# A four-layer kernel: norms and gates of the second layer as filling work, joined gate products, and loads and clears issued earlier

## The chip, the cores and the metric

The kernel runs on one core of one Trainium2 chip. The metric is device time in microseconds (us) of one execution, and for the kernel before it is a median over 17 runs. A separate profiled execution gives the trace that the line numbers, durations and windows come from. The engines are named PE (TensorE, matrix products; PEld is its weight load), DVE (VectorE), ACT (ScalarE), POOL (GpSimd) and SP (SyncE, which here only issues DMAs).

## The reference, cut to what matters

The input is 16 sequences of 256 tokens with 128 channels, 4096 tokens in all. Four layers follow one another, each of the form

```
xn = layernorm(x)
x  = x + attn(xn) + ffn(xn)
```

The first layer (called layer 0 here) has a recurrence over the 256 tokens of a sequence: a 64 x 128 memory matrix per sequence is updated and normalised at every token. The change is mostly in the second (layer 1):

```
# attn, on the 16 sequences of 256 tokens
n  = channel_group_norm(xn, 16 groups)        # over (8 channels x 256 tokens)
q, k = l2_normalize(n @ qw.T), l2_normalize(n @ kw.T);  v = n @ vw.T
y  = 16 heads of 8: ((q k^T) * scale * gamma_h^(i-j), causal) v
x1 = xn + y @ ow.T + ob
x2 = x1 + silu(channel_group_norm(x1) @ w1.T + b1) @ w2.T + b2

# ffn: four experts, a number of them per token between 1 and 4
h      = relu(xn @ dp_w1 + dp_b1)
ent    = softplus(h @ dp_w2 + dp_b2)
k_tok  = clip(round(1 + clip((ent - 0.5) / 1.5, 0, 1) * 3), 1, 4)
logits = xn @ gate_w + gate_b
w      = softmax over the k_tok largest logits, 0 elsewhere
out    = sum_e w_e * (relu(xn @ ew1_e + eb1_e) @ ew2_e + eb2_e)
```

The third layer (layer 2) has a windowed attention with a memory and eight experts of fixed capacity; the fourth (layer 3) softmax attention and eight experts with one expert per token. Layer 2 adds into a DRAM table `acc_d` and layer 3 scatters rows into a DRAM table `xs_d`. Both tables have to be zero before that.

## The kernel before, in words

X, the running sum, stays on the chip as 32 tiles of 128 tokens. The layers run one after another.

**Layer 0** ends with a recurrence of 16 chunks of 16 steps (index c for the chunk, t for the step), a chain that passes between DVE and ACT, with the other engines beside it; a chunk takes about 35 us. For each chunk SP issues loads from DRAM: VA and KT (lines 726 and 730), CZ (699), CR (712), and small tables tw (717). An output projection (L1162, added into X at L1166) follows.

**Layer 1** (lines 1170 to 1551) starts with its weights: 26 DMAs on ACT's own queue (L1180 to L1217). Then it makes the layer norm of all 32 tiles in 8 groups of 4 (L1233 to L1240): `kit.stats` gives mean and variance on DVE (L122, L123) and the reciprocal root on POOL (L112, L113), `kit.normalise` writes xn on DVE (L143), PE transposes four tiles (L151), and ACT copies them to xnT (L1240).

After that a loop over the 32 tiles is a pipeline with its order written out by hand. For DVE, PE and ACT the order of the program text is the order of execution (`manual_schedule`); for POOL and SP a scheduler decides. Tile n passes these stages:

- `normed(g)`, once for each four tiles: a channel group norm (L1242 to L1271) in pieces, with small products pgn (L1251, L1260) and a power on POOL (L1263).
- `project(n)`: the product pq for q, k and v (L1349), squares on ACT (L1356), ss on POOL (L1359, L1360), qk on DVE (L1364), and the outer products kv on POOL (L1373).
- `retain(n, h)` for two halves of heads: the product pk with a triangular table (L1392; for odd tiles also with ones on the tile before, L1391), then pr and y on DVE (L1396, L1399). There are two buffers of pk.
- `turn(n)`: a transpose of y on PE into pyt (L1407).

Between these stages the loop calls `some(k)`, which takes k steps from a generator, the *filler*: 7 steps in each of the 33 iterations and 2 ahead of the loop. In the kernel before, the filler is first `gates()` and then eight `tail(g)`. `gates()` has 25 steps: for each of 8 groups one product ph (L1279, 64 columns, relu into hd by ACT at L1281), four products pl of xnT with gate_w (L1285) and four of hd with dp_w2 (L1288). The rest is one block: a copy of pl to lg (L1292), and a chain of small DVE and ACT operations to the weights W (L1294 to L1332). The 25th step transposes W (pw, L1337), copies it to WT and sends it to DRAM as w_d (L1339).

`tail(g)` has 24 steps for four tiles. It begins with DMAs that read w_d back, spread over the partitions as WB (L1414) and as w4 (L1416). Then come the experts' up products (L1425), relu on ACT (L1427), a multiplication by WB on DVE (L1428), down products (L1433), the attention's output and its feed-forward part, and the addition into X (L1491). `tail(g)` may not start before tile 4g + 3 is turned. An operation on DVE that follows a filler product (the multiplication by WB, say) is put into a list `St.later` and is emitted with the next step. What is left of the filler after the loop is drained.

**Preparation of layer 2.** `prepare2` is called before layer 1. Its loads are on SP's queue, its small memsets on POOL. At its end (L1619 to L1627) it makes a tile of zeros on POOL and clears `acc_d` (2048 KB) and `xs_d` (2967 KB) with two DMAs on SP's queue (L1622).

Of the kernel before, what the change touches and what calls it, by code (L numbers as in the profile page):

```python
# [9 lines left out]
F32 = mybir.dt.float32  # L10
# [14 lines left out]
NCH = T // CH  # L25

# [57 lines left out]
class Kit:  # L84


    def __init__(self, ctx, tc, tables):
# [12 lines left out]

        self.mv3 = pool.tile([P, NT, 2], F32, name="mv3")
# [13 lines left out]
    def stats(self, pool, src, n):  # L115
# [10 lines left out]
        return mv, rstd  # L126

# [38 lines left out]
def layer0(tc, I, kit, X):  # L166
# [3 lines left out]
    with ExitStack() as ctx:  # L170
# [462 lines left out]
        with ExitStack() as c2:  # L633
# [237 lines left out]
            def chunk(c):  # L871
# [53 lines left out]
                for t in range(CH):  # L925
# [35 lines left out]
                    if t in (9, 10):  # L961
                        shares(t - 9, SA, CR)
                    elif c > 1 and t in (4, 5, 6, 11, 12, 13, 14):
                        beside(320)
                    if c < 2 and t < 8 and t % 2:
                        gram_out(1, 4 * c + t // 2, Run.pgs, 0)
# [203 lines left out]
def layer1(tc, I, kit, X):  # L1170
    nc = tc.nc
    H, DH, E = 16, 8, 4
    with ExitStack() as ctx:
        wp = ctx.enter_context(tc.tile_pool(name="l1_w", bufs=1))
        big = ctx.enter_context(tc.tile_pool(name="l1_big", bufs=1))
# [3 lines left out]
        for i, n in enumerate(("qw", "kw", "vw")):  # L1179
            nc.scalar.dma_start(wqkv[:, i, :], I[f"L1_attn_{n}_T"])  # L1180
        ow = wp.tile([P, D], F32, name="ow")
        nc.scalar.dma_start(ow, I["L1_attn_ow_T"])
        col = {}
        for n in ("norm_g", "norm_b", "ob", "ffn_norm_g", "ffn_norm_b"):
            col[n] = wp.tile([P, 1], F32, name="c_" + n)
            nc.scalar.dma_start(col[n], I["L1_attn_" + n].unsqueeze(1))
        w1 = wp.tile([P, 2 * D], F32, name="w1")
        nc.scalar.dma_start(w1, I["L1_attn_w1_T"])
        w2 = wp.tile([P, 2, D], F32, name="w2")
        nc.scalar.dma_start(w2, I["L1_attn_w2_T"].rearrange("(k p) d -> p k d", p=P))  # L1190
        b1 = wp.tile([P, 2], F32, name="b1")
        nc.scalar.dma_start(b1, I["L1_attn_b1"].rearrange("(k p) -> p k", p=P))
        b2 = wp.tile([P, 1], F32, name="b2")
        nc.scalar.dma_start(b2, I["L1_attn_b2"].unsqueeze(1))

        gw = wp.tile([P, E], F32, name="gw")
        nc.scalar.dma_start(gw, I["L1_ffn_gate_w"])
        gb = wp.tile([P, E], F32, name="gb")
        nc.scalar.dma_start(gb, row_bcast(I["L1_ffn_gate_b"]))
        dw1 = wp.tile([P, 64], F32, name="dw1")  # L1200
        nc.scalar.dma_start(dw1, I["L1_ffn_dp_w1"])
        db1 = wp.tile([64, 1], F32, name="db1")
        nc.scalar.dma_start(db1, I["L1_ffn_dp_b1"].unsqueeze(1))
        dw2 = wp.tile([64, 1], F32, name="dw2")
        nc.scalar.dma_start(dw2, I["L1_ffn_dp_w2"])
        db2 = wp.tile([P, 1], F32, name="db2")
        nc.scalar.dma_start(db2, row_bcast(I["L1_ffn_dp_b2"]))
        ew1 = wp.tile([P, E, 2 * D], F32, name="ew1")
        nc.scalar.dma_start(ew1, I["L1_ffn_ew1"].rearrange("e d h -> d e h"))
        ew2 = wp.tile([P, E, 2, D], F32, name="ew2")  # L1210
        for e in range(E):
            nc.scalar.dma_start(ew2[:, e], I["L1_ffn_ew2"][e].rearrange("(k p) d -> p k d", p=P))
        eb1 = wp.tile([P, E, 2], F32, name="eb1")
        with nc.allow_non_contiguous_dma(reason="1024 biases"):
            nc.scalar.dma_start(eb1, I["L1_ffn_eb1"].rearrange("e (k p) -> p e k", p=P))
        eb2 = wp.tile([E, D], F32, name="eb2")
        nc.scalar.dma_start(eb2, I["L1_ffn_eb2"])  # L1217
# [8 lines left out]
        kvp = ctx.enter_context(tc.tile_pool(name="l1_kv", bufs=3))  # L1226
# [5 lines left out]


        for g in range(8):
            sl = slice(4 * g, 4 * g + 4)
            mv, rstd = kit.stats(tmp, X[:, sl, :], 4)
            xn = tmp.tile([P, 4, D], F32, name="xn")
            kit.normalise(xn, X[:, sl, :], mv, rstd, 4)
            pn = kit.transpose4(ps2, xn, "h")
            nc.scalar.copy(xnT[:, 512 * g : 512 * g + 512], pn)  # L1240

# [31 lines left out]
        def gates():  # L1273

            pl = ps.tile([P, NT, 8], F32, name="pl", tag="f")
            for g in range(8):
                cols = slice(512 * g, 512 * g + 512)
                ph = ps2.tile([64, 512], F32, name="ph", tag="h")
                nc.tensor.matmul(ph, dw1, xnT[:, cols], start=True, stop=True)  # L1279
                hd = tmp.tile([64, 512], F32, name="hd")  # L1280
                nc.scalar.activation(hd, ph, AF.Relu, bias=db1)  # L1281
                yield
                for i in range(4):
# [1616 lines left out]
```

## Time and profile before

| | us |
|---|---|
| median of 17 runs | 1955.23 |
| lowest and highest of them | 1950.46, 1959.74 |
| profiled execution, its own time | 1955.67 |
| its span in the trace | 1953.7 |
| last part of layer 0's sum into X (L1166) | 656 |
| first copy to xnT (L1240) | 674.72 |
| first product pq (L1349) | 686.09 |
| last product pl | 734.9 |
| transpose of W (L1337) | 746.44 |
| last addition into X of layer 1 (L1491) | 1016.4 |

The page gives for each engine the share of the span in which it was busy: PE 77%, DVE 69%, ACT 42%, POOL 33%. These are averages over four layers with different limits, so a change in one layer is read from that layer's rows. A *window* is a stretch of the span, with each engine's busy time (and number of instructions), the mean clock that PE was granted (1.00 is full speed), the share of time in which the DMA engines were busy, and GB/s. The *chain of waits* is followed back from the last instruction: at each step it goes to what released the instruction, or to the instruction before it on its engine. SP's *timeline* lists when it issues DMAs: start, duration of the issue, line, and destination<-source; the transfer itself comes later.

### The profile page before, as it was taken

The page shows a single profiled execution, that of the slowest core. Times are in us where ns is not written, and L with a number is a line of the kernel's source. Part 1 is how long each engine was busy: PE and PEld are TensorE (multiplying, and loading weights), DVE is VectorE, ACT ScalarE, POOL GpSimd, SP SyncE. Part 2 cuts the span into 40 slices and gives each one's busy share as a digit, 9 for nine tenths or more (in the row PEclk, how much of TensorE's full clock was granted, in tenths as well). Part 3 has the DMA queues.
Part 4 walks back from the last instruction along what each step waited for, and adds up shares of the span by engine and source line. Part 5 has one row for each costly group of instructions (what it writes and reads, how often), then busy time and mean ns, then how long its engine had stood idle before and what let it go on. Part 6 is the DMA issues. An engine that isn't in the chain of part 4 may idle for free.

```text
span 1953.7 us, 26353 instructions
## 1 busy us (share of the span) xinstructions
PE 1510.9 (77%) x8176; PEld 920.6 (47%) x8176; DVE 1340.3 (69%) x4656; ACT 822.5 (42%) x1908; POOL 636.5 (33%) x901
## 2 busy tenths in 40 slices
PE   6676666766765598999988888687887289999995
PEld 3355455554654453444434454344444145555553
DVE  5688999888898537887855567654366256666663
ACT  3554554555555113232324345343443044454443
POOL 4332313122121223343413031566672713333310
PEclk9676767777676668999998999898888589999998
DMA  3130001000000451101102000022222313333314
GB/s 106 26 86 21 14 12 48 17 12 16 11 16 3 99 96 52 37 22 44 22 0 43 4 1 1 18 44 50 36 57 82 109 57 91 103 101 93 107 54 120
DMA packets 114978, 94.43 MB, mean 48 GB/s; under 512 B 35463, under 2 KB 97799, under 8 KB 114599
## 3 DMA queue, kind: packets, MB, share of 16 engines
q1 hardware_dynamic: 94172, 64.20, 13.0%
q0 software_dynamic: 13056, 26.21, 5.4%
q10 hardware_dynamic: 7610, 2.35, 0.5%
q8 instruction: 65, 1.06, 0.2%
q14 instruction: 75, 0.61, 0.1%
HBM read 55.65 MB, written 37.01 MB: 47 GB/s over the span
## 4 chain that ended last, share of the span: by engine, by line
PE 44%; DVE 11%; POOL 5%; issue 4%; DMA 2%; ACT 1%; another core or an unknown queue 0%; ACTq 0%; SPq 0%; POOLq 0%; DVEq 0%
PE pM L2606 6%; PE pc L2619 3%; PE ph L2282 3%; PE pf L1433 3%; PE pf L2265 3%; DVE mx L2781 3%; PE ph L1425 2%; PE pf L2708 2%; PE pk L1392 2%; PE tr L151 2%; PE ph L2701 2%; PE pk L1391 1%; POOL tok L2168 1%; DVE x L143 1%; PE pE L2606 1%
## 5 line engine op out<-in xcount | busy, mean ns | idle before, releaser
L2781 DVE TENSOR_REDUCE mx<-pM 128x4 f32<-128x1024 f32 x128 | 155.2, 1216 | 128.4 <-PE pE L2606 84.9
L2606 PE MATMUL pM<-ke,qe 31*128 31x256 f32 x1024 | 157.9, 436 | 69.8 <-DVE mx L2781 32.3
L2786 ACT ACTIVATE PT<-pE 128x1024 f32<-128x1024 f32 x128 | 130.4, 1024 | 170.1 <-PE pE L2606 168.3
L2606 PEld LDWEIGHTS pM<-ke,qe 31*128 31x128 f32 x1024 | 96.7, 201 | 112.6 <-DVE mx L2781 54.9
L2606 PE MATMUL pE<-qe,ke 32*128 32x256 f32 x1024 | 148.5, 410 | 0.6 <-ACT PT L2786 0.4
L940 ACT ACTIVATE SA<-e,y 16x1 f32<-16x1 f32 x256 | 74.9, 292 | 131.9 <-DVE e L939 104.6
L976 ACT ACTIVATE iR<-SA,A,CR 16x1 f32<-16x1 f32 x240 | 92.5, 386 | 53.2 <-DVE A L945 38.1
L808 PE MATMUL pP<-KB,M 128*128 128x64 f32 x224 | 59.7, 402 | 49.9 <-ACT M L690 49.9
L1131 POOL TENSOR_SCALAR KA<-KT,aS 128x128 f32<-128x128 f32 x128 | 74.8, 603 | 64.1 <-ACT aS L1103 64.1
L2606 PEld LDWEIGHTS pE<-qe,ke 32*128 32x128 f32 x1024 | 93.0, 189 | 4.5 <-ACT PT L2786 2.5
L740 POOL COPY KB<-K 64x256 f32<-64x256 f32 x30 | 11.9, 397 | 248.1 <-PE pP L808 247.3
L1373 POOL TENSOR_TENSOR kv<-qk,v 128x1024 f32<-128x1024 f32 x32 | 65.9, 2059 | 40.9 <-PE pf L1433 10.9
L808 PEld LDWEIGHTS pP<-KB,M 128*128 128x128 f32 x224 | 49.7, 297 | 59.0 <-ACT M L690 59.0
L1427 ACT ACTIVATE e<-ph,eb 128x512 f32<-128x512 f32 x64 | 44.1, 689 | 76.8 <-PE ph L1425 76.1
L2720 POOL DMA_INDIRECT ya_d<-yo,own x46 | 45.8, 995 | 80.8 <-DVE yo L2718 73.8
L2619 PE MATMUL pc<-PT,ve 128*32 128x256 f32 x1024 | 71.1, 397 | 0.0
L1399 DVE TENSOR_REDUCE y<-pr 128x64 f32<-128x512 f32 x64 | 69.1, 1080 | 2.2
L292 PE MATMUL pn<-tab,xn 128*128 128x128 f32 x32 | 14.3, 460 | 70.7 <-POOL xn L284 70.7
L1392 PE MATMUL pk<-kv,tab 128*128 128x512 f32 x128 | 68.4, 626 | 0.0
L1425 PE MATMUL ph<-xnT,ew 128*128 128x512 f32 x128 | 66.8, 603 | 0.0
L1433 PE MATMUL pf<-e,ew 128*128 128x512 f32 x128 | 64.1, 592 | 0.0
L945 DVE SCALAR_TENSOR_TENSOR A<-CR,e,A 16x33 f32<-16x33 f32 (+3 forms) x240 | 57.6, 240 | 8.5
(603 smaller groups left out, 4202.9 us busy)
## 6 DMA issues: line engine op xcount, KB each, us to landing
WB<-w_d SPq DMA_DIRECT2D x8, 1024.0 KB
c_d<-cs SPq DMA_DIRECT2D x16, 512.0 KB
ew<-in_L_ffn_W SPq DMA_DIRECT2D x16, 256.0 KB
xs_d<-zero SPq DMA_DIRECT2D x1, 2967.0 KB
xt<-xs_d POOLq DMA_DIRECT2D x23, 129.0 KB
xrow_d<-XN SPq DMA_DIRECT2D x4, 548.0 KB
X<-in_x SPq DMA_DIRECT2D x4, 512.0 KB
VA<-v_d SPq DMA_DIRECT2D x64, 32.0 KB
```

Source lines behind the costliest of these rows:

```text
L808: nc.tensor.matmul(Run.pP[p // 4][:, o : o + 64], M[:, p, :], KB[:, p].rearrange("q h k -> q (h k)"), start=p % 4 == 0, stop=False, skip_g ...
L940: nc.scalar.activation(s, e, AF.Sqrt, bias=y, scale=-1.0)
L976: nc.scalar.activation(iR, s, AF.Sqrt, bias=A[:, 17:18], scale=SB[:, t, 17:18])
L1131: nc.gpsimd.tensor_scalar(KA[:, p, :], KT[:, p, :], Run.aS[:, p : p + 1], None, ALU.mult)
L1392: nc.tensor.matmul(pkf, kit["triu"], St.kv[n][:, hs], start=i == 0, stop=True)
L1399: nc.vector.tensor_reduce(St.y[n][:, hh], pr.rearrange("p h e f -> p h f e"), AX.X, ALU.add)
L1425: nc.tensor.matmul(ph, ew1[:, e, k * P : (k + 1) * P], xg, start=True, stop=True)
L1433: nc.tensor.matmul(pf, ew2[:, e, k, :], he[q], start=False, stop=False)
L2606: nc.tensor.matmul(out[:, k, i, :], A[rows, s, c + i * P : c + i * P + P], B[rows, s, c : c + T], start=True, stop=True,)
L2619: nc.tensor.matmul(St.pc[32 * r : 32 * r + 32, s % 2, :], VEs[b % 2][:, k, 4 * s + r, :], St.PT[b, s][:, r, k, :], start=k == 0, stop=k == 1,)
L2781: vec.tensor_reduce(St.mx[bm][:, h0 : h0 + 2, :], pM, AX.X, ALU.max)
L2786: act.activation(St.PT[b, s][:, r0 : r0 + 2], pE, AF.Exp, scale=scale)
```

## The change

1. *Norms.* Only group 0's layer norm stays ahead of the loop. The moments are now made by an existing function (`kit.next_moments`, which leaves mean, reciprocal root and the negative of their product, the last with two small POOL operations more than before), the rows by `norm_rows` (two tiles on DVE, two on ACT), and the transposes and the copy by `norm_turn`. Groups 1 to 7 become the first 27 steps of the filler, `norms()`. `normed(g + 1)` starts at the second tile of a group of four rather than at the first.
2. *Gates.* gate_w is joined to dp_w1 as four more columns; ph has 68 rows, 64 through relu and 4 through identity with gate_b as bias, as two ACT operations. dp_w2 becomes a table of 68 x 5: an identity block for the four logits and dp_w2 as fifth column. So a group takes one ph and four pl rather than one and eight, and the addition of gate_b on DVE falls away. The products of a group come one round after its ph. The chain to W is cut by seven `yield`s, so the loop's own work comes between its pieces. `gates()` has 18 steps of products and 8 of the chain.
3. *Weights of layer 1.* The 26 DMAs are on SP's queue. The order in which layer 1's buffers are laid out changes, so that the weights take room that the recurrence's `work` buffers had. In SP's order they stand behind the last chunk's KT load. The joined tables take a few POOL operations (two memsets and a copy).
4. *Clears.* Both tables and the tile of zeros belong to the kit now. `kit.clear_rooms` is called in chunk 3 of layer 0's recurrence at step 9: a DVE memset of the zeros (128x129), and the two DMAs on SP's queue, between two tw loads.
5. *yT.* The copy of pyt to yT is made as soon as the fourth tile of a group is turned, with four buffers, not when the tail starts.

The diff, cut to its core:

```diff
+    def clear_rooms(self):
+        nc = self.nc
+        nc.vector.memset(self.zero, 0.0)
+        for rows, n, w in (
+            (self.acc_d.rearrange("(n p) c -> p n c", p=P), NT, D),
+            (self.xs_d.rearrange("(k p) c -> p k c", p=P), L3_NTL * L3_TS // P, D + 1),
+        ):
+            nc.sync.dma_start(rows, self.zero[:, 0:w].unsqueeze(1).to_broadcast([P, n, w]))
...
+                    if (c, t) == (3, 9):
+                        kit.clear_rooms()
...
-            nc.scalar.dma_start(wqkv[:, i, :], I[f"L1_attn_{n}_T"])
+            nc.sync.dma_start(wqkv[:, i, :], I[f"L1_attn_{n}_T"])
...
+        dw1 = wp.tile([P, 64 + E], F32, name="dw1")
+        nc.sync.dma_start(dw1[:, 0:64], I["L1_ffn_dp_w1"])
+        nc.sync.dma_start(dw1[:, 64:], I["L1_ffn_gate_w"])
...
+        dw2 = wp.tile([64 + E, E + 1], F32, name="dw2")
+        nc.gpsimd.memset(dw2[0:64], 0.0)
+        nc.gpsimd.memset(dw2[64:], 0.0)
+        nc.gpsimd.tensor_copy(dw2[64 : 64 + E, 0:E], kit.ident[64 : 64 + E, 64 : 64 + E])
+        nc.sync.dma_start(dw2[0:64, E : E + 1], I["L1_ffn_dp_w2"])
...
-        for g in range(8):
-            sl = slice(4 * g, 4 * g + 4)
-            mv, rstd = kit.stats(tmp, X[:, sl, :], 4)
-            xn = tmp.tile([P, 4, D], F32, name="xn")
-            kit.normalise(xn, X[:, sl, :], mv, rstd, 4)
-            pn = kit.transpose4(ps2, xn, "h")
-            nc.scalar.copy(xnT[:, 512 * g : 512 * g + 512], pn)
+        def norm_rows(g):
+            xn = xns[g] = tmp.tile([P, 4, D], F32, name="xn")
+            for i in range(4):
+                n = 4 * g + i
+                if i % 2 == 0:
+                    nc.vector.tensor_scalar(
+                        xn[:, i, :], X[:, n, :], kit.mv3[:, n, 0:1], kit.rs3[:, n : n + 1], ALU.subtract, ALU.mult
+                    )
+                else:
+                    nc.scalar.activation(
+                        xn[:, i, :], X[:, n, :], AF.Identity, scale=kit.rs3[:, n : n + 1], bias=kit.nb3[:, n : n + 1]
+                    )
+        def norms():
+            for g in range(1, 10):
+                if g < 8:
+                    kit.next_moments(tmp, X, g)
+                yield
+                if 2 <= g < 9:
+                    norm_rows(g - 1)
+                yield
+                if g >= 2 and g < 9:
+                    norm_turn(g - 1)
+                yield
...
-            for g in range(8):
+            for g in range(9):
+                if g < 8:
...
+                    ph = ps2.tile([64 + E, 512], F32, name="ph", tag="h")
+                    nc.tensor.matmul(ph, dw1, xnT[:, cols], start=True, stop=True)
+                    hd = tm2.tile([64 + E, 512], F32, name="hd")
+                    nc.scalar.activation(hd[0:64], ph[0:64], AF.Relu, bias=db1[0:64])
+                    nc.scalar.activation(hd[64:], ph[64:], AF.Identity, bias=db1[64:])
                 yield
-                for i in range(4):
-                    ts = slice((4 * g + i) * P, (4 * g + i + 1) * P)
-                    nc.tensor.matmul(pl[:, 4 * g + i, 0:E], xnT[:, ts], gw, start=True, stop=True)
+                if g > 0:
+                    for i in range(4):
+                        n = 4 * g - 4 + i
+                        nc.tensor.matmul(pl[:, n, 0 : E + 1], last[:, i * P : (i + 1) * P], dw2, start=True, stop=True)
                 yield
...
         def filler():
+            yield from norms()
             yield from gates()
...
+            kit.next_moments(tmp, X, 0)
+            norm_rows(0)
+            norm_turn(0)
             for _ in normed(0):
                 pass
...
-                if j == 0 and g + 1 < 8:
+                if j == 1 and g + 1 < 8:
                     norm = normed(g + 1)
...
-    clear(acc_d.rearrange("(n p) c -> p n c", p=P), NT, D)
-
-    xs_d = dram.tile([L3_NTL * L3_TS, D + 1], F32, name="xs_d")
-    clear(xs_d.rearrange("(k p) c -> p k c", p=P), L3_NTL * L3_TS // P, D + 1)
```

## The prediction

> **What bounds the kernel now.** I read the page's head and clock row first, then the chain of waits around the seam of layers 0 and 1, the rows of the xnT copy, the windows from 656 us on, and SyncE's timeline for the clears.
>
> ```profile
> span 1953.7 us, 26353 instructions
> ...
> PEclk9676767777676668999998999898888589999998
> ```
>
> The profiled execution took 1955.67 us, 0.44 above the median of the 17 runs; the sum is made against it. Each digit of the clock row is 48.8 us; layer 1 (656 to 1016.4 us) begins in the 14th, and the 14th and 15th stand at 6 where its later ones stand at 9.
>
> ```profile
> 656.74 2.58 DMA wqkv<-in_L_attn_vw_T
> ...
> 672.20 2.49 DMA fl<-in_L_attn_fgate
> 674.72 0.59 ACT xnT L1240
> ...
> 686.09 1.65 PE pq L1349 x2
> ...
> 746.01 0.39 DVE W L1332
> 746.44 0.47 PE pw L1337
> ```
>
> The chain (start, duration) runs through weight transfers until ScalarE makes its first copy at 674.72, then through the other norms to the first projection at 686.09, and at 735 to 746 through the gate chain.
>
> ```profile
>   DMA fl<-in_L_attn_fgate: 28.7, 1
> ```
>
> This is the idle time before that copy. ScalarE was issuing 26 weight DMAs (655.85 to 674.6). The first norm's rows were ready at 660, so this wait is pure queueing.
>
> ```profile
> core 0: us, PE busy (x) PEld busy (x) DVE busy (x) ACT busy (x) POOL busy (x), PEclk, DMA share, GB/s
> 656.00:686.00 30.00, 9.32 (x36) 6.79 (x36) 20.23 (x111) 4.59 (x8) 12.61 (x65) 0.50 0.72 148
> 686.00:698.00 12.00, 11.91 (x26) 5.91 (x27) 2.59 (x10) 3.15 (x12) 5.78 (x6) 0.50 1.15 221
> 698.00:735.00 37.00, 37.00 (x146) 21.58 (x144) 13.57 (x26) 6.01 (x17) 6.43 (x7) 0.76 0.32 37
> 714.00:738.00 24.00, 24.00 (x100) 13.15 (x99) 9.38 (x17) 6.18 (x17) 5.08 (x6) 0.86 0.00 1
> 754.00:1016.00 262.00, 256.75 (x680) 115.77 (x679) 206.05 (x443) 82.46 (x219) 91.80 (x93) 1.00 0.12 30
> ```
>
> PE is the bound from 686 to 735 (37.00 of 37 busy) but slow: 0.50, then 0.76. From 754 it is 98% busy at full clock.
>
> ```profile
> 681.00 0.53 SPq L1622 DMA_DIRECT2D acc_d<-zero  x1
> 681.58 5.43 SPq L1622 DMA_DIRECT2D xs_d<-zero  x1
> 747.24 0.33 SPq L1339 DMA_DIRECT2D w_d<-WT  x1
> 748.84 0.36 SPq L1414 DMA_DIRECT2D WB<-w_d  x1
> ```
>
> The two clears move 5.0 MB; the DMA view shows their traffic ending near 706, about 25 us after issue. The last two lines are the way of the gate weights into WB.
>
> **The change, part by part.** A filler step is one piece of second work; a loop iteration (one tile of 128 tokens) takes seven, and two lie before the loop.
>
> *Start of layer 1.* The 26 issues leave ScalarE and seven norms leave the front. What remains before the first pq, from 656.3: moments 1.1, 45 POOL memsets (end 657.2, they stay), rsqrt 1.3, two rows on DVE 0.56 beside two on ACT, four transposes 1.2, copy 0.59, then the group norm (DVE pieces 3.2, two small products, pow 0.7): about 11.7 with waits. First pq at 668 instead of 686.1. The weights now stand in SP's queue after the KT load of the last chunk and wait only for that chunk's products, so they are issued about 617 to 632, with 25 us to land; the recurrence hides them. SP's later preparation of layer 2 started at 655.84, when its buffers came free, and is no later. Bounds: 666 to 676.
>
> *Part A, 27 norm steps* (3.6 iterations). DVE: 7 x (1.1 + 0.56) = 11.6; retain 2 x (0.684 + 1.081) and qk 0.68 per tile, 3.4 tiles: 14.3; one group norm 3.2; together 29. PE at full clock: a tile costs 3.8 (pq 0.81, triangular pk 1.8, half of the tiles another 1.9 of pk, pyt 0.3), x 3.6 = 13.6, transposes 7 x 0.6 = 4.2: 18; at half clock 36. POOL: 3.6 x (kv 1.96 + ss 0.93) + 7 x (1.27 + two small 0.5) = 23, with one wait for SP's late fl load (about 670) ahead of the fourth rsqrt. So A lies between 29 (DVE) and 42 (half clock and waits); since 656 to 698 ran at 0.50, I take 35.
>
> *Part B, 18 product steps* (2.57 iterations). The 32 logit products (64 passes, L1285) go; the logits ride as four more columns in ph and pl. ACT gets 8 more activations (at most 0.68 each; ACT was busy 9 of 49 us here, so hidden). PE at full clock: 8 ph x 1.0 + 8 quads of pl x 0.98 + 2.57 x 3.8 = 25.6; at half clock 51. With the clock between the rows 0.76 and 0.86, 0.81, B is 31.5. Bounds 26 and 48.
>
> The Trainium skill, "TensorE: Matmul & The Clock Gate", Part 1, What's actually happening, says that about 3.4 us of sustained work release the throttle. The trace differs: PE was 11.91 of 12 busy at 0.50, and the measurement decides. By the rule B would be near 26 and the time about 1943.
>
> *Part C, 8 steps of the gate chain* (1.14 iterations). Before, it ran as one block from lg at 735.8 to pw at 746.44 with PE idle. It loses one add (0.29); between its pieces now stand 1.14 tiles of DVE work (4.8) and pieces of a group norm (1.4): 10.3 + 6.2 = 16.5 to pw. Bounds 13 (DVE busy alone: 6 + 6.2, and some waits) and 18.
>
> *A new wait.* WB lands about 9 us after w_d's issue (747.24 to the WB traffic's end, 756). Before, tails began with tile 5 and two tiles' work lay between. Now eight tiles are turned, tail 0 starts at once, and its first e*WB stands on DVE with the next pr and y behind it; with two pk buffers PE stops too. PE has about 5 us of other work: 4 us (0 to 6).
>
> *The rest.* Before: 753.6 to 1016.4 = 262.8 for tiles 5 on and eight tails. Now tails start at about 7.3, back to back (before, 4 of 28 steps were empty): 2.3 tiles x 3.8 = 8.7 less, 254.1. The yT copy is the same, only earlier.
>
> *Clears in chunk 3.* One DVE memset (POOL took 0.21 for the same form) may sit on the recurrence: 0.2. The DMAs are issued near 215, land near 241 at the seam's 25.5 us; the tw loads queued behind them on SP and the rings are needed near 247.5. Hidden by chunk 4's first eight steps, with 6 us over; without it up to 8. SP issues in order and some completion counters are shared, so CR (222.79 before), KT (233.38) and CZ (238.30) behind the clears also wait for their landing and leave near 241; KT is first read by POOL's KA after 250 and CZ with the next chunk, so they stay hidden too. At 681 they delayed nothing that PE waited for, so their leaving gains 0.
>
> The Trainium skill, "DMA: Bandwidth & Descriptors", Issuing engines are not separate DMA queues, says that another issuing engine saves only the sequencer's time, usually small. Here that time was 28.7 us of idle ScalarE, so the trace disagrees with "small"; if the rule held, pq would come near 681 and the time near 1962.
>
> Sum: 668 + 35 + 31.5 + 16.5 + 4 + 254.1 = 1009.1, with the memset 1009.3, against 1016.4: 7.1 earlier. Layers 2 and 3 keep their work. 1955.67 - 7.1 = 1948.6.
>
> **Rivals.** (1) *The clock stays at half*, the other side. For: 0.50 over 656 to 698 with PE full in the last 12, and again in 702 to 714; A is DVE-bound and leaves PE gaps. Against: 0.86 from 714, while a cold PE is itself full in A. A 40, B 48: end 1030.8, time 1970. It decides from A + B = 73.6, a mean clock in B under 0.66.
> (2) *The clears hold the recurrence*: they land more than 32 us after issue. For: 134 to 175 GB/s in the second half of their transfer. Against: other loads shared that. Up to +8: 1956.
> (3) *All is better hidden*: A 29, B 26, C 14, no WB wait: end 991, time 1931. For: the 98% of 754 to 1016. Against: the clock rows.
> (4) *The start isn't freed*, because SP, which issues in order, reaches the weights late: pq near 676, time 1957. Against: in its timeline of before SP issued nothing from 612 to 641.
>
> **How the numbers follow.** Chances: forecast 0.50, (1) 0.18, (2) 0.08, (3) 0.16, (4) 0.08. What a measurement here can tell from no change is about 0.2%, 3.9 us. The forecast's own range is 1939 to 1957 (A 31 to 38, B 28 to 37): some 0.42 of it faster, 0.06 same, 0.02 slower. Adding (3) as faster, (1) as slower but 0.02, (2) and (4) spread over the three: faster 0.63, same 0.14, slower 0.23. The range takes in all of (3) and (2) and (4) and the lower half of (1): 1930 to 1966.
>
> **What would show it.** First pq near 668 with no ACT wait on a DMA; layer 1's last X add near 1009; PE busy 60% or more but DVE fuller in 668 to 703; clock of 0.8 in 703 to 735; a DVE wait on WB's DMA once, near 752 to 758; chunk 4 of the recurrence as long as chunk 5; pl with one shape only. Wrong if the first 70 us after pq take over 77 at a low clock, if KT or tw loads show up as releasers near 247, or if POOL's rsqrt ends the waits of A.

## The result and the profile after

The changed kernel takes 1964.03 us (median of 8 runs, 1961.99 to 1965.92), the kernel before 1955.63 (47 runs, 1949.82 to 1959.77). The ratio is 1.0045, 95% interval [1.0034, 1.0055]: 0.45% slower. The forecast was 1948.6, faster, and both the sign and the size were wrong; the time lies inside the range of 1930 to 1966 and near its upper end.

The traces agree on where it happens. Layers 2 and 3, from the last X add of layer 1 to the end of the span, take 937.3 us before (1953.7 - 1016.4) and 937.8 after (1962.6 - 1024.8). Layer 0's last add starts at 655.8 before and 656.6 after. So the loss is in layer 1: from that add to its own last X add it took 360.6 us and takes 368.2.

The head and the clock row of the page of the kernel after:

```profile
span 1962.6 us, 26250 instructions
...
PEclk9676767777676688989998999898988589999997
```

The chain of waits of the kernel after, from layer 0's end to the first tail (start, duration, what):

```profile
662.45 0.59 ACT xnT L1274
...
668.36 1.66 PE pq L1401 x2
...
715.37 0.86 PE ph L1327 x2
...
754.38 0.49 PE pw L1389
...
757.13 7.96 DMA w<-w_d
765.14 2.07 PE pf L1509 x2
```

The first projection comes at 668.4, 17.7 us earlier than before, as forecast. But the first product of the gates stands at 715.4, 47 us later; that was to be 35. The gate weights W are transposed at 754.4 (8 us later than before), and after it PE waits for w4 to come back from DRAM.

The windows of the kernel after that belong to the norm steps, the product steps, and two stretches further on (columns as in the header):

```profile
core 0: us, PE busy (x) PEld busy (x) DVE busy (x) ACT busy (x) POOL busy (x), PEclk, DMA share, GB/s
668.00:715.00 47.00, 31.23 (x68) 14.44 (x69) 33.27 (x110) 13.96 (x46) 27.24 (x46) 0.59 0.12 15
715.00:737.00 22.00, 22.00 (x106) 13.22 (x104) 11.72 (x23) 13.98 (x32) 5.77 (x6) 1.00 0.00 0
...
825.00:845.00 20.00, 17.88 (x45) 8.39 (x44) 13.95 (x35) 4.53 (x14) 5.14 (x7) 0.83 0.10 25
...
870.00:880.00 10.00, 9.34 (x23) 4.25 (x22) 8.43 (x25) 2.91 (x8) 4.48 (x5) 0.83 0.00 1
```

Beside the norm steps neither PE (31 of 47) nor DVE (33 of 47) is full, at a clock of 0.59. The product steps then run at full clock without a gap; in the kernel before, 698 to 735 stood at 0.76. In 825 to 845 and 870 to 880 PE has gaps and its clock drops, in a part of the layer where the kernel before was 98% busy at 1.00.

The waits of the kernel after between 735 and 772 (total, times, longest):

```profile
DVE e L1482 <- DMA WB<-w_d: 6.4, 1, 6.4
...
PE pf L1509 <- DMA w<-w_d: 4.7, 1, 4.7
```

This is the new wait behind W: DVE's first multiplication by WB, and PE's product with w4.

SP's timeline of the kernel after, around the clears in chunk 3:

```profile
214.14 0.38 SPq L143 DMA_DIRECT2D acc_d<-zero  x1
214.58 5.01 SPq L143 DMA_DIRECT2D xs_d<-zero  x1
219.68 14.15 SPq L734 DMA_DIRECT2D tw<-rec_d  x2
234.11 1.72 SPq L747 DMA_DIRECT2D KT<-kh_d  x4
235.94 0.36 SPq L729 DMA_DIRECT2D CR<-rec_d  x1
241.36 0.31 SPq L716 DMA_DIRECT2D CZ<-rec_d  x1
```

CZ waits 5.0 us for the landing of the second clear and leaves at 241.4 (238.3 in the kernel before). CR leaves at 235.9 instead of 222.8, now behind the KT loads; the wait found for it is 0.9 us on DVE and none on a clear, so the prediction's reading that CR and KT would be held until 241 did not come true. The waits of the recurrence (36 to 600 us) name one load in the kernel after, GB with 1.1 us (2.2 before), and neither KT nor tw.

### The profile page after: what moved, and what is told of

It is laid out like the page before. It is cut to its first block, busy times and chain, and to the rows that moved or that the text cites. A ratio compares the mean times of both kernels' runs of the same rounds, so it can differ in the third digit from the quotient of the medians.

```text
span 1962.6 us, 26250 instructions
## 1 busy us (share of the span) xinstructions
PE 1501.7 (77%) x8112; PEld 913.2 (47%) x8112; DVE 1341.9 (68%) x4640; ACT 833.7 (42%) x1932; POOL 636.3 (32%) x919
## 4 chain that ended last, share of the span: by engine, by line
PE 42%; DVE 13%; issue 4%; POOL 4%; DMA 2%; ACT 1%; another core or an unknown queue 0%; SPq 0%; POOLq 0%; DVEq 0%; ACTq 0%
PE pM L2651 6%; PE pc L2664 3%; PE pf L1487 3%; DVE mx L2826 3%; PE ph L1479 3%; PE ph L2327 2%; PE pf L2310 2%; PE pf L2753 2%; PE pk L1444 2%; PE ph L2746 2%; PE tr L168 2%; DVE x L160 1%; POOL tok L2213 1%; PE pk L1443 1%; PE pE L2651 1%
## 5 line engine op out<-in xcount | busy, mean ns | idle before, releaser
L757 POOL COPY KB<-K 64x256 f32<-64x256 f32 x30 | 11.8, 394 | 247.1 <-PE pP L825 246.3
L1425 POOL TENSOR_TENSOR kv<-qk,v 128x1024 f32<-128x1024 f32 x32 | 64.8, 2024 | 35.6 <-DVE qk L1416 19.5
L1482 DVE TENSOR_TENSOR e<-e,WB 128x512 f32<-128x512 f32 x64 | 45.8, 715 | 28.5 <-ACT e L1481 21.9
```

## The experiments

The runs were made on several chips, on which the kernel before took medians of 1921 to 1960 us; what follows layer 1 takes 902 to 905 us on some and 934 to 940 on others, whatever the kernel. Layer 1 itself does not depend on the chip in the one case that shows it: front, filler and chain are the same to 0.1 us in the changed kernel and in tails_aligned, which ran on different ones. So times are compared as ratios to the kernel before on the same chip, and the stages by their lengths in each trace. All lengths in us, from one trace for each kernel, with marks rounded to 0.1. "Front" is from the start of layer 0's last add to the first pq, "filler" from there to the copy of pl to lg (norm steps, if any, and product steps), "chain" from lg to pw, "rest" from pw to the last X add of layer 1.

| run | front | filler | chain | rest | layer 1 | ratio [95%] |
|---|---|---|---|---|---|---|
| before | 30.3 | 49.7 | 10.6 | 270.0 | 360.6 | 1 |
| after | 11.8 | 68.7 | 17.3 | 270.4 | 368.2 | 1.0045 [1.0034, 1.0055] |
| norms_ahead | 24.6 | 26.8 | 19.5 | 273.9 | 344.8 | 0.9907 [0.9877, 0.9938] |
| tails_aligned | 11.8 | 68.7 | 17.3 | 261.5 | 359.3 | 0.9966 [0.9945, 0.9987] |
| weights_only | 50.2 | 50.8 | 10.7 | 272.5 | 384.2 | 1.0125 [1.0086, 1.0165] |
| gates_only | 30.8 | 29.2 | 11.8 | 274.3 | 346.1 | 0.9911 [0.9874, 0.9948] |
| norms_dense | 11.7 | 49.3 | 15.7 | 273.8 | 350.5 | 0.9971 [0.9956, 0.9985] |
| moments_ahead | 22.0 | 61.9 | 17.3 | 270.3 | 371.5 | 1.006 [1.0043, 1.0077] |
| chain_block | 24.6 | 26.8 | 12.8 | 277.8 | 342.0 | 0.9922 [0.9905, 0.9938] |
| weights_clears | 31.3 | 55.4 | 10.6 | 270.1 | 367.4 | 1.0037 [1.0023, 1.0052] |
| pl_twice | 24.5 | 33.8 | 12.9 | 277.7 | 348.9 | 0.9948 [0.9931, 0.9964] |
| gates_beside | 44.4 | 2.6 | 10.5 | 291.3 | 348.8 | 0.9938 [0.9921, 0.9955] |
| rank_beside | 44.4 | 2.6 | 7.5 | 293.0 | 347.5 | 0.9926 [0.9904, 0.9948] |
| xnT_passes | 24.6 | 38.2 | 10.5 | 273.5 | 346.8 | 0.9942 [0.9921, 0.9964] |
| no_lag | 24.6 | 46.1 | 10.6 | 280.9 | 362.2 | 1.0019 [1.0, 1.0038] |
| front_and_rank | 25.9 | 25.0 | 10.8 | 277.4 | 339.1 | 0.9889 [0.9863, 0.9915] |

A filler with more steps leaves fewer tiles for the rest, so "filler" and "rest" are to be read together: 7 steps are one tile, 3.8 us of PE at full clock.

### norms_ahead: the norms out of the filler

```diff
-            kit.next_moments(tmp, X, 0)
-            norm_rows(0)
-            norm_turn(0)
+            for g in range(9):
+                if g < 8:
+                    kit.next_moments(tmp, X, g)
+                if g > 0:
+                    norm_rows(g - 1)
+                    norm_turn(g - 1)
...
         def filler():
-            yield from norms()
             yield from gates()
```

> The changed kernel with all eight layer norms ahead of the loop again (moments and rows in the changed form, each group's rows and transposes one group behind its moments) and no norm steps in the filler. Theory 1, the norm steps in the filler are dear (47 us for 3.57 iterations where the tiles alone take 3.57 x 3.8 = 13.6) and through their 27 steps they push the tails out of their phase: first pq near 678 (13 us of DVE moments and rows, then 7 for the group norm), tail 0 starts with tile 4 as in the kernel before, last X add of layer 1 near 1000, time about 1939 (1933 to 1946). Rival: the joined products, the split chain or the moved loads cost the time: last X add at 1018 or later, time 1957 or more.

Measured: first pq at 680.1, last X add at 1000.3, ratio 0.9907. Theory 1 gave 678 and 1000, and the rival falls. Taking this one part back (with the norms in the changed kernel's form, each group's moments ahead of the rows of the group before) makes layer 1 23.4 us shorter than in the changed kernel and 15.8 shorter than in the kernel before. The front is 12.8 us longer than in the changed kernel, and the filler 41.9 shorter.

### tails_aligned: the tails in one phase

```diff
-                while St.turned < 4 * g + 3:
+                while not (St.turned >= 4 * g + 3 and (St.ended or St.fresh and St.turned % 4 == 3)):
```

(`St.fresh` is set for the one step after a turn, `St.ended` after the loop.)

> The changed kernel, but a tail starts only at the step at which it could start in the kernel before (right after the last tile of a group of four is turned), so tails come every 28 steps, one group later, and two of them are drained after the loop. Theory 1: back-to-back tails run against the tile stages in changing phases, and that costs the 10 us that the stretch 825 to 912 has too much: tile spacing of 35 us per four tiles all along, PE 98% busy at full clock from 765 on, last X add near 1014, time about 1953 (1949 to 1957). Rival: what is lost there is not the phase but work that must be done anyway, and the second drained tail costs 3 us more: last X add 1025 to 1029, time 1964 to 1968.

Measured: last X add at 1016.2 (forecast 1014; 1024.8 without the alignment), the rest 261.5 instead of 270.4. Windows of this run:

```profile
797.00:832.00 35.00, 34.05 (x92) 15.37 (x91) 28.77 (x63) 10.47 (x30) 13.84 (x14) 1.00 0.12 31
832.00:867.00 35.00, 34.05 (x92) 15.28 (x90) 28.86 (x63) 10.51 (x30) 13.89 (x14) 1.00 0.14 30
867.00:902.00 35.00, 33.91 (x92) 15.60 (x92) 28.38 (x63) 10.68 (x31) 13.84 (x14) 1.00 0.13 28
```

The drops of the clock are gone, although tail 0 starts later and two tails are drained after the loop. PE's waits for DVE's statistics are not: from 797 to 1002 they are 4.4 us here and 3.9 in the changed kernel. The edit also starts tail 0 later, and that shortens the wait for the gate weights: PE waits 1.2 us for w4 instead of 4.7, DVE 1.6 for WB instead of 6.4. The first 20 us from the transpose of W on, in the changed kernel and in this run:

```profile
754.00:774.00 20.00, 14.94 (x29) 6.70 (x30) 9.24 (x23) 3.90 (x10) 3.75 (x5) 0.75 0.43 109
754.00:774.00 20.00, 16.38 (x39) 7.09 (x40) 15.46 (x38) 4.70 (x15) 7.98 (x7) 0.91 0.41 110
```

Busy time multiplied by the clock is an estimate of the work that PE did, in us at full clock: 11.2 and 14.9. So some 3.7 of the 8.9 us stand beside the wait, and only the other 5 or so in the later windows, where the phase differs.

### norms_dense and moments_ahead: what is dear in the norm steps

In norms_dense a group's moments, the rows of the group before and its transposes make one step:

```diff
                 if g < 8:
                     kit.next_moments(tmp, X, g)
-                yield
                 if 2 <= g < 9:
                     norm_rows(g - 1)
-                yield
-                if g >= 2 and g < 9:
                     norm_turn(g - 1)
                 yield
```

> The changed kernel with the norms still in the filler, but a whole group (moments, rows of the group before, its transposes) in one step: 9 steps instead of 27. Theory 1a, what is dear is the number of loop iterations that run beside the norms, each about 13 us long there because its chain (ScalarE, POOL, DVE, POOL, PE) is exposed, and the phase of the tails that follows: first pq 668, first ph near 690 instead of 715, tail 0 starts with tile 4 or 5, last X add 1000 to 1007. Rival 1b, the norms' own work on DVE and POOL is what costs, wherever it stands in the filler: first ph 705 or later, last X add 1015 or later.

Measured: first pq 671.7, first ph 698.3, last X add 1010.5. Layer 0 ended 3.4 us later here than in the changed kernel, so the last two are 694.9 and 1007.1 on the clock of the forecast: the upper end of what theory 1a gave for the add, the ph 5 later than it gave; the rival's 705 and 1015 are not reached.

In moments_ahead the moments of all groups go ahead of the loop, and the 27 steps stay:

```diff
             kit.next_moments(tmp, X, 0)
             norm_rows(0)
+            for g in range(1, 8):
+                kit.next_moments(tmp, X, g)
             norm_turn(0)
...
-                if g < 8:
-                    kit.next_moments(tmp, X, g)
                 yield
```

> The changed kernel with the moments of all groups ahead of the loop (28 more pairs of bn_stats and bn_aggr on DVE, and POOL's 7 x 4 small operations, start there), while rows and transposes stay in the 27 filler steps. Theory 1c, POOL's order is the cause (the tile's ss and kv stand behind rsqrt work that waits for DVE, and DVE's qk behind ss): first pq near 676, and the norm steps take 30 us or less instead of 47, first ph at 706 or earlier, last X add near 1013. Rival 1a, the exposed chain of each iteration and the half clock: the steps still take 39 us or more, first ph at 715 or later, last X add 1022 or later.

Measured: first pq 678.3, first ph 718.4, last X add 1027.8. From pq to ph it is 40.1 us instead of 46.8, 6.7 less, and the front is 10.2 longer: the 7.7 us of DVE moments (7 x 1.1) are merely moved, with nothing won. Theory 1c (POOL's order) falls.

Together the three lengths from pq to ph give the price. 27 steps took 46.8, 9 steps with the same norm work 26.6: 18 steps, or 2.57 iterations, cost 20.2 us, 7.9 each, about twice the 3.8 of full clock. Of the 26.6, 1.3 iterations at that price are 10, and the other 16 are near the norms' own DVE work, 11.6 of moments and rows and 3.2 of a group norm. The window of norms_dense that holds them:

```profile
672.00:698.00 26.00, 13.77 (x38) 6.63 (x38) 22.17 (x81) 11.32 (x31) 17.88 (x36) 0.54 0.21 24
```

So the tile work and the norm work add up. The chain of waits from the first pq to the first ph, added up by engine, shows it too: in the changed kernel PE 18.8, DVE 17.9, POOL 6.4, ScalarE 1.9 and issue 2.0 us; in norms_dense PE 5.8, DVE 11.4, POOL 6.3, ScalarE 0.8 and issue 2.4. The work passes from one engine to the next, and no engine bounds the stretch alone. PE is busy 31 of 47 us and 14 of 26, at a clock of 0.59 and 0.54 (27 of 40 at 0.69 in moments_ahead). Of the 20.2 us that the 18 steps cost, 13.1 are PE's and 6.4 DVE's, so it is in part chance that 7.9 is close to a tile's price on PE at half clock.

### weights_only and weights_clears: the queue and the clears

In weights_only only the queue changes, and the order in which the buffers are laid out; in weights_clears the clears go to chunk 3 too, and the layout is that of the change.

```diff
-            nc.scalar.dma_start(wqkv[:, i, :], I[f"L1_attn_{n}_T"])
+            nc.sync.dma_start(wqkv[:, i, :], I[f"L1_attn_{n}_T"])
```

> The kernel before with the 26 weight DMAs of layer 1 on SP's queue and its buffers laid out as in the change; nothing else. Theory 1: ScalarE's first copy to xnT goes from 674.7 to about 660, the eight norms are then bound by DVE (8 x 2.2 = 18 us), first pq near 679 instead of 686, and the 7 us reach the end: time about 1948 to 1949. Rival: the norms' DVE work and the clock hide it, first pq at 684 or later and time 1953 or more.

> The kernel before with the weight DMAs on SP in the buffer layout of the change, and with the two clears in chunk 3 of the recurrence: the queue change and the move of the clears together, norms and gates as before. Theory: now the weights stand behind the last chunk's loads and no longer behind the 5 MB of clears, ScalarE's first copy comes near 661, the norms are bound by DVE, first pq near 679, and the end of layer 1 is 7 us earlier than before (ratio 0.9965). Rival: first pq 684 or later, or a longer recurrence, ratio 0.999 or more.

Both expectations failed. In weights_only the first pq comes at 711.4, the layer is 23.6 us longer and the kernel 1.25% slower. SP's timeline of that run shows why:

```profile
679.64 0.53 SPq L1622 DMA_DIRECT2D acc_d<-zero  x1
680.22 5.43 SPq L1622 DMA_DIRECT2D xs_d<-zero  x1
685.70 14.86 SPq L1181 DMA_DIRECT2D wqkv<-in_L_attn_qw_T  x1
...
709.25 0.33 SPq L1187 DMA_DIRECT2D c_ffn_norm_g<-in_L_attn_ffn_norm_g  x1
```

With this layout the weights were not free early; they stand behind layer 2's loads and the 5 MB of clears, and c_ffn_norm_g leaves only when xs_d has landed. So the queue change needs the move of the clears, or the change's own layout with one more pool of buffers, which weights_only lacks; weights_clears has both, and no run tells them apart.

In weights_clears the weights are there in time, ScalarE's first copy comes at 663.7, 5.3 us after layer 0's last add instead of 18.9, and nothing is won: the front is 31.3 us instead of 30.3. From its chain of waits (the longest pieces between 669 and 690):

```profile
671.53 1.12 DVE xn L159 x4
673.65 1.05 POOL rstd L120
674.72 1.12 DVE xn L159 x4
677.91 1.11 DVE xn L159 x4
```

The norm loop of the kernel before is a round trip of 3.2 us per group: moments on DVE, root on POOL, rows on DVE, and only then the next group's moments. Eight of them are 25.5 us, so the front is about as long as in the kernel before, whose chain ran through ScalarE's DMAs. In norms_ahead, where the moments of the next group stand before the rows of this one and half of the rows are on ScalarE, the front is 24.6. In weights_clears the filler is also 5.7 us longer than before: PE stays at half clock for longer,

```profile
690.00:720.00 30.00, 30.00 (x80) 17.65 (x80) 6.87 (x19) 5.40 (x19) 7.45 (x10) 0.50 0.00 1
```

with no DMA traffic beside it, so a low clock here does not need the clears' traffic beside it.

### gates_only, pl_twice, xnT_passes, no_lag: the product steps and the clock

gates_only is the kernel before with the joined products (the diff of the change, chain kept as a block).

> The kernel before with the gate products joined (one ph of 68 columns and four pl of five for each group, two activations); the chain stays one block, norms, weights and clears stay where they were. Theory 1: the 64 passes of the logits (10.7 us busy in the profile before) go from a stretch that PE bounds: last X add 9 us earlier, time about 1946 to 1948. Rival: with fewer products PE is granted its full clock later, and half of it is lost again: 4 us, time 1951.

Measured: the filler 29.2 instead of 49.7, the last X add at 1003.4, ratio 0.9911. The gain is 14.5 us of layer 1 where theory gave 9: PE's clock is 0.89 in the second ten us after the first pq and 1.00 after that. Which of the joined form's features does that? Three runs start from chain_block (below), whose filler is 26.8.

```diff
-                        nc.tensor.matmul(pl[:, n, 0 : E + 1], last[:, i * P : (i + 1) * P], dw2, start=True, stop=True)
+                        for _ in range(2):
+                            nc.tensor.matmul(pl[:, n, 0 : E + 1], last[:, i * P : (i + 1) * P], dw2, ...)
```

> The kernel of the run chain_block with each of the 32 pl products issued twice into the same place (64 more passes of five columns, the number that the kernel before has). Theory: passes with so few columns are what keeps the granted clock at half, although PE is shown as busy without a gap; then the stretch from the first pq to the lg copy (26.8 us in chain_block, at full clock from its tenth us on) runs at 0.50 for 20 us or more and takes 42 to 55. Rival: the clock does not care, the passes cost their 8 x 0.8 = 6.4 us: 33 us.

Measured 33.8, clock 0.90 and then 1.00: the rival's 33. The number of short passes does not hold the clock down.

```diff
+                if g > 0:
+                    for i in range(4):
+                        n = 4 * g - 4 + i
+                        nc.tensor.matmul(pl[:, n, 5:8], xnT[:, n * P : (n + 1) * P], dw1[:, 64:67], start=True, stop=True)
+                yield
```

> The kernel of the run chain_block with 64 more passes as the kernel before has them: xnT as weights (128 x 128) and three columns moving, into columns of pl that nobody reads, as a step of its own in each round (8 steps more). Theory: it is these passes (other weights, full 128 rows) that keep the granted clock at half in the kernel before; from the first pq to the lg copy, with 1.1 iterations more than in chain_block, 45 us or more, clock 0.50 for 20 us after the first pq. Rival: the clock comes up after 10 us as in chain_block: 26.8 + 6.4 + 1.1 x 3.8 = 37 to 39.

Measured 38.2 (rival: 37 to 39). The removed passes cost their own time and do not hold it down either.

```diff
-            for g in range(9):
-                if g < 8:
+            for g in range(8):
...
-                        nc.tensor.matmul(pl[:, n, 0 : E + 1], last[:, i * P : (i + 1) * P], dw2, start=True, stop=True)
+                    nc.tensor.matmul(pl[:, n, 0 : E + 1], hd[:, i * P : (i + 1) * P], dw2, start=True, stop=True)
```

> The kernel of the run chain_block with the pl products of a group right after its own ph, as in the kernel before, instead of one round later. Theory: pl then waits for ScalarE's two activations, PE has short gaps the whole stretch, and these keep the granted clock at half: first pq to lg copy 40 or more, where chain_block took 26.8. Rival: two fewer steps and no effect on the clock: 25 to 28.

Measured 46.1, as the theory gave (40 or more). Windows of no_lag:

```profile
684.00:694.00 10.00, 8.42 (x16) 3.66 (x16) 0.93 (x4) 3.27 (x13) 3.56 (x5) 0.50 0.01 2
694.00:704.00 10.00, 7.12 (x20) 4.32 (x20) 2.37 (x4) 2.71 (x4) 2.23 (x2) 0.50 0.00 1
704.00:714.00 10.00, 8.48 (x18) 3.73 (x17) 2.77 (x6) 2.19 (x4) 0.00 (x0) 0.50 0.00 0
```

and of chain_block:

```profile
682.00:692.00 10.00, 8.99 (x20) 3.98 (x21) 1.86 (x6) 4.61 (x14) 5.09 (x6) 0.61 0.01 2
692.00:702.00 10.00, 10.00 (x49) 6.14 (x49) 5.86 (x12) 6.33 (x13) 2.64 (x4) 1.00 0.00 0
```

and the wait in no_lag between 686 and 730:

```profile
PE pl L1333 <- ACT hd L1329: 7.6, 6, 1.5
```

With pl right behind its own ph, PE stops six times for ScalarE's hd, none longer than 1.5 us, 7.6 in all. The clock stays at 0.50 for the first 30 us, and the stretch takes 19.3 us longer, with two filler steps fewer. So the distance between ph and pl is what brings the clock up; that the short waits themselves hold it down fits this pair of runs, but weights_clears shows 0.50 without any. One round of distance between ph and pl, a detail of the change that the forecast gave no price, is worth more than the removed passes.

### chain_block, gates_beside, rank_beside, front_and_rank: towards a faster version

chain_block is norms_ahead with the yields inside the gate chain taken out.

> All norms ahead of the loop, as in the run norms_ahead, and the gate chain as one block (the yields inside it taken out). Theory: splitting the chain gains nothing, since DVE and ScalarE run in order and the tile work between the pieces only makes the chain longer; the block ran 12.2 us in gates_only and the split chain 19.8 us in norms_ahead: last X add near 997, time 3 us below norms_ahead. Rival: the tile work between the pieces has to be done anyway and now starts later: last X add 1002 or later.

Measured: layer 1 in 342.0 instead of 344.8, 2.8 us less, the chain 12.8 instead of 19.5. The split gains nothing. The ratios, from different chips, do not show the 2.8 us: 0.9922 and 0.9907, with intervals that overlap.

gates_beside puts the 18 product steps beside the norms ahead of the loop:

```diff
+                if g >= 2:
+                    next(gate)
+                    next(gate)
```

> The kernel of the run chain_block with the 18 product steps of the gates taken out of the loop and put beside the norms ahead of it (ph of a group two groups behind its moments, pl three behind), and the first group norm in pieces between them. Theory: ahead of the loop DVE is the bound (24 us with PE busy 10.6), so the products (16 us at full clock, 32 at half) mostly fit beside it: last X add 8 us earlier than in chain_block counted from the end of layer 0 (342 us there), 334. Rival: PE is at half clock there and becomes the bound, and the chain's block then stands ahead of tile 0 with nothing beside it: 340 to 346.

The rival was right and still too kind: 348.8. The front becomes 44.4 with PE at 0.50 throughout, and the first tiles then run with no filler beside them.

rank_beside adds a new order of the chain (ranks while ScalarE makes the entropy, the exponential before the entropy's last steps):

> The kernel of the run gates_beside with the ranks of the logits, which do not need the entropy, computed on DVE while ScalarE works on it, and the exponential issued before the entropy's last steps. Theory: the block from lg to W waits 5 to 6 us for ScalarE (table loads of 1.28 three times); about 4 of them go: last X add 3 to 4 us earlier than in gates_beside. Rival: tile work fills that gap by now: less than 1 us.

The chain goes from 10.5 to 7.5 and the layer from 348.8 to 347.5: 1.3 us, between the theory and the rival. Of the 3.0 us that the chain is shorter, the rest takes 1.7 back, and the intervals of the two ratios overlap.

front_and_rank is chain_block with that order of the chain and the first group norm in pieces between the norms.

> A version meant to be faster: the kernel of the run chain_block (all norms ahead in pipelined order, the gate chain one block), with the first group norm in pieces between the norms and the ranks computed while ScalarE works on the entropy. First pq 2 to 3 us earlier, the block 4 us shorter: layer 1 from layer 0's last add to its own last X add 336 to 339 instead of 342, ratio to the kernel before 0.988 to 0.991. Rival: tile work fills both gaps and nothing is gained, 341 or more, ratio 0.992.

Layer 1 takes 339.1, ratio 0.9889 [0.9863, 0.9915]: 1.1% faster than the kernel before, the shortest layer 1 and the lowest ratio here. The intervals of norms_ahead, gates_only and chain_block overlap it: the joined products alone (gates_only, 0.9911) bring most of what can be had. The chain gave 2.0; the front did not get shorter (25.9 against 24.6), so putting the group norm between the norms won nothing there.

## Why the prediction was wrong

**Start of layer 1** (668): first pq at 668.4, right in size. The reason given for part of it was wrong: the 28.7 us for which ScalarE waited on a DMA were read as queueing that the end pays for. Only 18.8 of them were spent on issues (655.85 to 674.6); the rest is idle time of ScalarE before layer 1. weights_clears takes the wait away and the front stays at 31 us, because the norms' round trip over POOL takes 25.5 us beside it. So the move of the weights alone gains nothing. With one norm left in the front the issues would probably have been in the way (an estimate from the 18.8 us of issues and the front of 11.8), but no run moves the norms and leaves the weights on ScalarE.

The Trainium skill, "DMA: Bandwidth & Descriptors", Issuing engines are not separate DMA queues, says that another issuing engine saves only the sequencer's time, usually small. In weights_clears that time was saved and was not small: ScalarE's first copy comes 13.6 us earlier after layer 0's end. None of it reached the first pq.

**Part A, norm steps** (35, bounds 29 to 42): 46.8, above both bounds, 11.8 too little. The step that failed is the choice between DVE's 29 and PE's 36 at half clock. They were taken as two engines side by side, so that the larger bounds the stretch; they add up. The work itself was priced well: PE's busy time times the clock, 31.2 x 0.59, is 18.4 us against the 18 of the forecast, and DVE was busy 33 against 29. But the chain of waits holds 18.8 us of PE, 17.9 of DVE, 6.4 of POOL, 1.9 of ScalarE and 2.0 of issue one after another. The engines hand the same few tiles to each other in program order, and none gets ahead; norms_dense, with 18 filler steps fewer beside the same norm work, is 20.2 us shorter.

**Part B, product steps** (31.5): 21.9, 9.6 too much, below the lower bound of 26. The prediction took the clock from the same stretch of the kernel before (0.76 and 0.86). The stretch ran at 1.00, since pl now stands one round behind ph; no_lag shows what it costs without. It was below the 25.6 of full clock because that sum adds up busy times that overlap. The groups of the changed kernel from 715 to 737 have nearly the same busy times, 8.2 for ph and 7.8 for pl, but all of PE's groups there add up to more than 26 us in a stretch of 22:

```profile
L1327 PE MATMUL ph<-xnT,dw 128*68 128x512 f32 x16 | 8.2, 600 | 0.0
L1335 PE MATMUL pl<-dw,hd 68*128 68x5 f32 x64 | 7.8, 246 | 0.0
```

The Trainium skill, "TensorE: Matmul & The Clock Gate", Part 1, What's actually happening, lets about 3.4 us of sustained work release the throttle. The prediction set it aside, because the trace showed PE 11.91 of 12 busy at 0.50. In chain_block PE's last wait ends at 686.3, and the clock is 0.50 until 689, 0.58 in the next us and 1.00 from 690: some 3.5 us, which agrees. In no_lag PE shows about 5 us of work between one wait and the next (688.9 to 694.0, for example), and the clock stays at 0.50; after the last wait, which ends at 714.6, it is 0.89 from 719 to 720. In weights_clears 30 us without a visible wait were not enough. So the rule came out in one run and not in the others. That PE in the kernel before waits like that of no_lag, hidden by the modelled ends of its matmuls, is possible but not shown: its trace has no PE wait on hd.

**Part C, the chain** (16.5): 17.3, right. But nothing was won by splitting it: chain_block needs 12.8 where norms_ahead needs 19.5, and its layer is 2.8 us shorter.

**The new wait** (4): 4.7 of PE on w4 and 6.4 of DVE on WB, the place and the size right. That the clock would be at 0.75 in the 20 us around it was not in the sum.

**The rest** (254.1 after the wait): pw to the last add was forecast as 4 + 254.1 = 258.1 and took 270.4, 12.3 too little. The step that failed is "tails start at about 7.3, back to back (before, 4 of 28 steps were empty): 2.3 tiles x 3.8 = 8.7 less". It took PE to run on at full speed while the tails closed up. The tile work did leave: by windows of ten us from pw to the last add, PE's busy time times its clock (an estimate of its work at full clock) adds up to 262.7 before and 248.7 after, 14.0 less. But PE was idle for 13.2 us there instead of 5.8, and its busy time at clocks under 1.00 cost 8.5 instead of 1.5, together 14.4 more, of which the sum had 4 as the new wait. tails_aligned, which puts the empty steps back, has the same PE work (249.0), 11.0 us of idle time and 1.5 by the clock, and needs 261.5. So what it wins is mostly clock (7.0 of some 9). Some 3.7 us of the whole stand beside the wait for the gate weights, and most of the rest in the two windows at 0.83. Why the clock falls in those two is not shown: a tail's DVE work (res, statistics, multiplications by WB) probably meets pr, y, z and the next group norm in a different order for each tail, and PE stops for it.

**Clears** (0.2): layer 0 ended at 656.6 against 655.8. Over the runs it ended at 655.5 to 661.6 with early clears and at 655.8, 657.3 and 661.2 without, so no cost can be told. They landed near 241, as estimated, and rival 2 did not occur.

The errors add up to the miss: 0.4 for the start, + 11.8 - 9.6 + 0.8 + 12.3 = 15.7, against 1024.8 - 1009.3 = 15.5; the 0.2 between them is the term for the memset. A and B together took 68.7 us, under the 73.6 up to which the prediction still had the change faster; that they came near the forecast's 66.5 is luck, a sum taken for a maximum in A against overlapping busy times and a low clock in B. So the sign was turned by the rest, where closing up the tails was taken to be free. The rival on the other side (a half clock in A and B) was right for A alone.

## What to carry to other kernels

Work moved from a front into a hand-ordered pipeline is not hidden because two engines each have room: price it as a sum until a trace shows an overlap, and count the iterations it adds at the clock that the emptier PE will be granted. A product that reads what another engine makes from the product just before it should stand a round later: without that the stretch took 19 us longer here, with 7.6 us of waits and the clock at 0.50 for 30 us. Before an idle wait is counted as a gain, look for the chain that ran beside it and was just as long. Do not count empty filler steps as time to be had: closing them up cost PE, with the wait for the gate weights, 14.4 us in idle time and clock, as much as the work that had left.

## What was not expected of the hardware

In no_lag PE waits six times between 686 and 730, at most 1.5 us each and 7.6 in all, and the granted clock stayed at 0.50 for 30 us; with nearly the same products and pl a round later it was 1.00 from the eighth us on (chain_block). 64 more short passes, of five columns or of three with other weights, did not change that (pl_twice, xnT_passes). In weights_clears PE is shown 30.00 of 30 busy at 0.50 with no DMA traffic beside it, so a full row of PE in a profile does not promise a full clock.
